# Eight-layer attention and expert kernel on one core: the last attention's batches started five steps apart, its LayerNorm and gates without exponentials, and the last experts emitted among the tails

## The chip, the cores and the metric

The kernel runs on one core of one Trainium2 chip. A core has five engines, each with its own instruction stream that it works off in order: TensorE (PE: matmuls and weight loads), VectorE (DVE), ScalarE (ACT: activation functions and copies), GpSimd (POOL), and SyncE (SP), which here only issues DMAs. They wait for each other through semaphores. The metric is the device time of one execution in microseconds (us); lower is better.

## The reference, cut to what matters

The model is four pairs of cross-attention and feed-forward over x of shape (4, 512, 128); each adds to x the result of a layer on the LayerNorm of x. The change touches the last pair (L3) only: attention over 32 context rows with 16 heads, and a top-2 mixture of 8 experts that evaluates every expert on every token.

```python
def _layernorm(x, axis=-1, eps=1e-05):
    m = jnp.mean(x, axis=axis, keepdims=True)
    v = jnp.var(x, axis=axis, keepdims=True)
    return (x - m) / jnp.sqrt(v + eps)

def _L3_xattn_ref(x, y, mask, wq, bq, wk, bk, wv, bv, wo, bo):
    ...  # q from x, k and v from y, split into 16 heads
    scores = jnp.einsum('bhqd,bhkd->bhqk', q, k) / np.sqrt(D_K)
    scores = scores + (1.0 - mask[:, None, None, :]) * -10000.0
    attn = jax.nn.softmax(scores, axis=-1)
    z = jnp.einsum('bhqk,bhkd->bhqd', attn, v)
    return z.transpose(0, 2, 1, 3).reshape(b, -1, d) @ wo.T + bo

def _L3_ffn_ref(x, router_w, w1, b1, w2, b2):
    logits = xf @ router_w.T
    probs = jax.nn.softmax(logits, axis=-1)
    top_v, top_i = jax.lax.top_k(probs, TOP_K)                      # TOP_K = 2
    gates = top_v / (jnp.sum(top_v, axis=-1, keepdims=True) + 1e-09)
    for e in range(E):                                              # E = 8
        ge = jnp.sum(jnp.where(top_i == e, gates, 0.0), axis=-1, keepdims=True)
        h = jax.nn.gelu(xf @ w1[e] + b1[e], approximate=False)
        out = out + ge * (h @ w2[e] + b2[e])

x = x + _L3_xattn_ref(_layernorm(x), ctx_1024, ...)
x = x + _L3_ffn_ref(_layernorm(x), ...)
```

## The kernel before

**Tiling.** The 2048 tokens are four batches g0 to g3 of 512 tokens; a batch is an x tile of 128 partitions by 4 token blocks (NJ) by 128 features, kept on the core throughout. Transposed activations are 128 x 512. Each of the eight PSUM tiles is 128 x 512 float32.

**Stages of the last pair.** The L2 experts end with scatters of their rows to DRAM. Then each batch goes through one chain:

- `combine2(g)`: two loads of the L2 results (tile `yg`, SP's queue), eight multiply-adds on DVE (L1152).
- `attend3(g)`, the attention: LayerNorm (statistics L194, L195 on DVE; one over the root through Ln and Exp on ACT, L199 and L200, and one Newton step on DVE, L204 to L207; the result written by ACT, L221), transposes on PE (L235) and their copy out of PSUM by ACT (L237). Then four rounds, one for each block of 128 tokens: scores (PE, L387), maximum and subtraction (DVE, L372 and L373), Exp (ACT, L374), four transposes (PE, L400), copy (ACT, L402), product with the values (PE, L406), division by the sum (DVE, L415 and L416). At the end transposes of the result (L235, L237), output projection (PE, L247) and addition to x (DVE, L459).
- `route3(g)`: LayerNorm again, this time written by DVE (L225), transposes (L235, L237), router matmul (L566), logits copied out by DVE (L572).
- `gate(g)`: top two of eight logits by comparisons on DVE, two Exps on ACT (L1196, L1197), and ten small DVE operations that make the gates.

After all four chains come the experts, batch after batch: the gates transposed (L1219, copied by ACT at L1221) and multiplied with the second biases (L247, added at L459), and then for each of eight experts two matmuls with 512 columns (L1227), two Gelus (L1228, ACT), eight matmuls of 128 columns (L1232) and four multiply-adds into x (L1242, DVE). A batch that is done is stored to `out`.

**What sets the order.** Chains are Python generators. `together` takes them in turns: in every step each running chain emits its work up to its next `yield`, and `skew` or `late` says in which step a chain starts. A scheduler then builds each engine's stream from that emission order, moving instructions where its own estimate of readiness says so. On the chip each engine works its stream off strictly in that order. In the last pair, batch g starts in step 2g (`skew` 2), and the experts are emitted by a plain loop after `together` has ended.

**ACT's function tables.** Ln and Exp are in one table set, Gelu in another. `exp_ln_tables()` loads the first at set places; the load for Gelu goes ahead of the first Gelu.

Of the kernel before, what the change touches and what calls it, by code (L numbers as in the profile page):

```python
# [8 lines left out]
F32 = mybir.dt.float32  # L9
I32 = mybir.dt.int32  # L10
# [57 lines left out]
def tile_kernel(ctx: ExitStack, tc: tile.TileContext, I, out):  # L68
# [141 lines left out]
    def normed(src, tag, plus=0.0, act=False, p=P, n=NJ, bufs=B, pool=wk):  # L210

        mv, r = yield from moments(src, p, n)
        y = pool.tile([P, n, D], F32, tag=tag, name=tag, bufs=bufs)
        if plus or act:
            c = small(n, "c")[:p]
            nc.vector.scalar_tensor_tensor(c, mv[:, :, 0], -1.0, r, ALU.mult, ALU.mult)
            if plus:
                nc.vector.tensor_scalar(c, c, plus, None, ALU.add)
        for j in range(n):
            if act:  # L220
                nc.scalar.activation(y[:p, j, :], src[:, j, :], AF.Identity, bias=c[:, j : j + 1], scale=r[:, j : j + 1])  # L221
            elif plus:
                nc.vector.tensor_scalar(y[:p, j, :], src[:, j, :], r[:, j : j + 1], c[:, j : j + 1], ALU.mult, ALU.add)
            else:
                nc.vector.tensor_scalar(  # L225
                    y[:p, j, :], src[:, j, :], mv[:, j, 0:1], r[:, j : j + 1], ALU.subtract, ALU.mult
                )
        yield
        return y
# [134 lines left out]
        nc.scalar.copy(vw[:rows], pt[:rows])  # L364
        return vw

    def softmax_terms(e, src, nh, n):

        e3 = e.rearrange("p (h n) -> p h n", n=n)
        src3 = src.rearrange("p (h n) -> p h n", n=n)  # L370
        mx = small(nh, "mx")
        nc.vector.tensor_reduce(mx, src3, AX.X, ALU.max)  # L372
        nc.vector.tensor_tensor(e3, src3, bc(mx, 2, n), ALU.subtract)  # L373
        nc.scalar.activation(e, e, AF.Exp)  # L374
        return e3

    def attend(xT, keys, values, g, H, n):
# [6 lines left out]
        for j0 in range(0, NJ, npb):  # L384
# [8 lines left out]
                )  # L393
            yield
            e = wk.tile([P, 512], F32, tag="att", name="att", bufs=B)
            softmax_terms(e, pt, npb * H, n)
            yield
            pt = psum()
            for k in range(4):
# [150 lines left out]
        return chain  # L550


    def routed(tag, w, bias=None, copies=()):


        xn, xnT = [None] * B, [None] * B
        logits = rk.tile([P, NT, NEXP], F32, tag=f"L{tag}", name="logits")

        def chain(g):
            xn[g] = yield from normed(X[g], "xn")  # L560
            for xd in copies:
                nc.sync.dma_start(xd[g * S : (g + 1) * S].rearrange("(j p) d -> p j d", p=P), xn[g])
            xnT[g] = yield from transposed(xn[g])
            pt = psum()
            for j in range(NJ):
                nc.tensor.matmul(  # L566
                    pt[:, j * P : (j + 1) * P], lhsT=xnT[g][:, j * P : (j + 1) * P], rhs=w, start=True, stop=True
                )
# [612 lines left out]
        return chain  # L1181


    def l3_ffn(xnT, logits, f3w1, f3w2, before, fetch):
        gates = [None] * B

        def gate(g):
            L = logits[:, g * NJ : (g + 1) * NJ, :]
            m1, oh1 = argmax(L, NJ)
            m2, oh2 = argmax(without(L, oh1, NJ), NJ)  # L1190

            z = rt.tile([P, NJ, NEXP], F32, tag="z", name="z", bufs=2)
            nc.vector.tensor_tensor(z, L, bc(m1, 2, NEXP), ALU.subtract)
            p2 = rt.tile([P, NJ], F32, tag="p2", name="p2", bufs=B)
            nc.vector.tensor_tensor(p2, m2, m1, ALU.subtract)
# [3 lines left out]
            p1 = rt.tile([P, NJ], F32, tag="p1", name="p1", bufs=B)  # L1199
            nc.vector.tensor_reduce(p1, z, AX.X, ALU.add)  # L1200
            nc.vector.reciprocal(p1, p1)
            nc.vector.tensor_tensor(p2, p2, p1, ALU.mult)
            den = rt.tile([P, NJ], F32, tag="den", name="den", bufs=2)
            nc.vector.scalar_tensor_tensor(den, p1, 1e-9, p2, ALU.add, ALU.add)
            nc.vector.reciprocal(den, den)
            nc.vector.tensor_tensor(p1, p1, den, ALU.mult)
            nc.vector.tensor_tensor(p2, p2, den, ALU.mult)
            gates[g] = rt.tile([P, NJ, NEXP], F32, tag="gates", name="gates", bufs=B)
            nc.vector.tensor_tensor(gates[g], oh1, bc(p1, 2, NEXP), ALU.mult)
            second = rt.tile([P, NJ, NEXP], F32, tag="second", name="second", bufs=2)  # L1210
            nc.vector.tensor_tensor(second, oh2, bc(p2, 2, NEXP), ALU.mult)
            nc.vector.tensor_tensor(gates[g], gates[g], second, ALU.add)
            yield

        together([*(queue(before(g), gate(g)) for g in range(B)), fetch], 2)
        for g in range(B):
            pt = psum()
            for j in range(NJ):
                nc.tensor.transpose(pt[:NEXP, j * P : (j + 1) * P], gates[g][:, j, :], ident)  # L1219
            gT = ex.tile([NEXP, S], F32, tag="gT", name="gT", bufs=2)  # L1220
            nc.scalar.copy(gT, pt[:NEXP])  # L1221
            add_to(X[g], proj(gT, f3b2, k=NEXP), X[g])
            for e in range(NEXP):
                hT = ex.tile([P, 2, S], F32, tag="hT", name="hT", bufs=2)
                for f in range(2):
                    pt = psum()
                    nc.tensor.matmul(pt, lhsT=f3w1[:, e, f * P : (f + 1) * P], rhs=xnT[g], start=True, stop=True)  # L1227
                    nc.scalar.activation(hT[:, f, :], pt, AF.Gelu, bias=col["f3_b1"][:, 2 * e + f : 2 * e + f + 1])  # L1228
                pt = psum().rearrange("p (j d) -> p j d", j=NJ)
                for j in range(NJ):  # L1230
                    for f in range(2):
                        nc.tensor.matmul(  # L1232
                            pt[:, j, :],
                            lhsT=hT[:, f, j * P : (j + 1) * P],
                            rhs=f3w2[:, e, f, :],
                            start=f == 0,
                            stop=f == 1,
                        )
                for j in range(NJ):
                    xj = X[g][:, j, :]  # L1240
                    ge = gates[g][:, j, e : e + 1]
                    nc.vector.scalar_tensor_tensor(xj, pt[:, j, :], ge, xj, ALU.mult, ALU.add)  # L1242
            nc.sync.dma_start(out[g].rearrange("(j p) d -> p j d", p=P), X[g])

    exp_ln_tables()
    xd0 = dram.tile([NTOK, D], F32, tag="xd0", name="xd0")
# [70 lines left out]
    with tc.tile_pool(name="lx", bufs=1) as lx:  # L1317
# [14 lines left out]

# [168 lines left out]
```

## Time and profile before

| | |
|---|---|
| median of 3 runs | 688.15 us (685.5 to 688.87) |
| the profiled execution's own time | 687.35 us |
| its span, first to last instruction | 685.5 us |
| TensorE busy / weight loads | 515.2 us (75%) / 393.8 us (57%) |
| VectorE, ScalarE, GpSimd busy | 331.9 (48%), 239.0 (35%), 164.3 us (24%) |
| mean granted TensorE clock | 0.86 |

Busy shares are means over a program of many stages, so they don't say what one stage waits for. The parts of the profile that do are: the chain that ended last, which goes back from the last instruction to what released each step; the stretches, which give each engine's busy time, and TensorE's granted clock (1.00 is full speed, 0.50 half), in any piece of the span; and the instructions in order of time, with the idle time ahead of each in brackets and what ended it. In all of them the times are us from the start of the span. Rows of PE often count twice what the source does, because a float32 matmul is recorded as two.

### The profile page before, as it was taken

How to read it: one execution, taken by the hardware profiler on the slowest of the kernel's cores; microseconds unless marked ns; L12 is line 12 of the kernel's file. 1: busy time of each engine (PE TensorE's matmuls, PEld its weight loads, DVE VectorE, ACT ScalarE, POOL GpSimd, SP SyncE). 2: the span in 40 equal slices, each digit the busy share in tenths (PEclk: the TensorE clock that was granted, in tenths of full speed). 3: DMA queues.
4: the chain of work that ended last, by engine and by line, in shares of the span. 5: the costliest groups of instructions: out<-in, count | busy, mean ns of one | idle time of the engine just before them, and what ended most of it. 6: DMA issues, size and time to landing. Idle time of an engine off the chain costs nothing.

```text
span 685.5 us, 8856 instructions
## 1 busy us (share of the span) xinstructions
PE 515.2 (75%) x3051; PEld 393.8 (57%) x3051; DVE 331.9 (48%) x1382; ACT 239.0 (35%) x540; POOL 164.3 (24%) x203
## 2 busy tenths in 40 slices
PE   3668987449389697876261997990789789999996
PEld 2557765338366436765141785880468657676765
DVE  4687654644577405666800311213867853333332
ACT  2343646203147313342110221340655334343332
POOL 4333333435012001000076766541200000000000
PEclk9999999759669889975666999996599959999999
DMA  8900101212870063002021112118000000000000
GB/s 327 313 9 17 32 27 51 77 50 73 308 277 1 0 236 134 1 1 63 0 46 43 47 47 46 38 30 257 4 1 1 1 0 1 16 0 16 1 17 15
DMA packets 42990, 44.97 MB, mean 66 GB/s; under 512 B 5161, under 2 KB 31026, under 8 KB 42818
## 3 DMA queue, kind: packets, MB, share of 16 engines
q1 hardware_dynamic: 39442, 36.20, 15.9%
q0 software_dynamic: 3072, 6.30, 3.4%
q10 hardware_dynamic: 432, 1.92, 0.8%
q8 instruction: 24, 0.39, 0.2%
q14 instruction: 20, 0.16, 0.1%
HBM read 34.97 MB, written 9.44 MB: 65 GB/s over the span
## 4 chain that ended last, share of the span: by engine, by line
PE 51%; DVE 10%; ACT 4%; issue 4%; DMA 3%; POOL 3%; another core or an unknown queue 3%; DVEq 0%; POOLq 0%; ACTq 0%
PE pt L1232 8%; PE pt L1227 8%; PE pt L1126 5%; PE pt L1118 4%; PE pt L387 3%; PE po L406 3%; PE pt L235 3%; PE pt L997 2%; PE pt L454 2%; PE pt L566 2%; POOL yd L769 2%; PE pt L400 1%; DMA yd<-ye,to 1%; PE pt L247 1%
## 5 line engine op out<-in xcount | busy, mean ns | idle before, releaser
L1232 PEld LDWEIGHTS pt<-f3w,hT 128*128 128x128 f32 x512 | 65.6, 191 | 33.4 <-ACT hT L1228 19.0
L1242 DVE SCALAR_TENSOR_TENSOR x<-pt,gates,x 128x128 f32<-128x128 f32 x128 | 36.0, 344 | 83.0 <-PE pt L1232 83.0
L1228 ACT ACTIVATE hT<-pt,cols 128x512 f32<-128x512 f32 x64 | 44.0, 688 | 73.8 <-PE pt L1227 73.4
L1232 PE MATMUL pt<-f3w,hT 128*128 128x128 f32 x512 | 68.2, 276 | 0.9 <-ACT hT L1228 0.6
L1227 PE MATMUL pt<-xnT,f3w 128*128 128x512 f32 x128 | 67.0, 611 | 0.0
L1126 PE MATMUL pt<-f2w,hT 128*128 128x128 f32 x320 | 47.2, 305 | 21.5 <-ACT hT L1121 14.6
L1121 ACT ACTIVATE hT<-pt 128x384 f32<-128x384 f32 (+1 forms) x64 | 26.9, 438 | 102.9 <-PE pt L1118 37.2
L1126 PEld LDWEIGHTS pt<-f2w,hT 128*128 128x128 f32 x320 | 44.7, 214 | 26.8 <-ACT hT L1121 15.2
L760 POOL DMA_INDIRECT xg<-xd,inv x48 | 46.5, 969 | 43.7 <-DVE to L678 14.1
L769 POOL DMA_INDIRECT yd<-ye,to x48 | 47.2, 984 | 35.6 <-DVE ye L1133 16.1
L235 PE MATMUL pt<-cst,xn 128*128 128x128 f32 x96 | 25.4, 362 | 38.7 <-ACT xn L221 20.9
L1133 DVE COPY ye<-pt 128x384 f32<-128x384 f32 (+1 forms) x16 | 7.9, 491 | 83.5 <-PE pt L1126 42.0
L235 PEld LDWEIGHTS pt<-cst,xn 128*128 128x128 f32 x96 | 15.6, 167 | 50.6 <-ACT xn L221 26.3
L194 DVE BATCH_NORM_STATS2 st<-x 128x6 f32<-128x128 f32 x128 | 32.3, 271 | 22.2 <-POOL x L547 16.1
L1118 PE MATMUL pt<-exT,f2w 128*128 128x256 f32 (+1 forms) x128 | 38.7, 445 | 0.0
L237 ACT COPY xnT<-pt 128x512 f32<-128x512 f32 x40 | 23.2, 586 | 42.5 <-PE pt L235 42.1
L400 PE MATMUL pt<-cst,att 128*128 128x128 f32 x128 | 21.0, 287 | 12.3 <-ACT att L374 12.3
L374 ACT ACTIVATE att<-att 128x512 f32<-128x512 f32 x32 | 20.0, 631 | 27.5 <-DVE att L373 27.3
L387 PE MATMUL pt<-keys,xnT 128*128 128x256 f32 (+1 forms) x64 | 28.1, 546 | 0.8 <-ACT xnT L237 0.7
L1118 PEld LDWEIGHTS pt<-exT,f2w 128*128 128x128 f32 x128 | 23.7, 196 | 7.7 <-issue 0.6
L406 PEld LDWEIGHTS po<-v,aT 128*128 128x128 f32 x192 | 25.1, 201 | 4.9 <-issue 3.5
L372 DVE TENSOR_REDUCE mx<-pt 128x16 f32<-128x512 f32 (+1 forms) x32 | 21.7, 683 | 12.8 <-PE pt L387 12.4
(323 smaller groups left out, 1024.4 us busy)
## 6 DMA issues: line engine op xcount, KB each, us to landing
e_w<-in_e_w SPq DMA_DIRECT2D x8, 512.0 KB, 7.3
e_wg<-in_e_wg SPq DMA_DIRECT2D x8, 512.0 KB, 8.0
yg<-yd SPq DMA_DIRECT2D x12, 256.0 KB, 4.2
f0w<-in_f_w SPq DMA_DIRECT2D x1, 2048.0 KB, 13.2
yd<-zero SPq DMA_DIRECT2D x8, 256.0 KB, 3.6
ew<-in_e_w SPq DMA_DIRECT2D x8, 256.0 KB, 3.2
xd<-xn SPq DMA_DIRECT2D x8, 256.0 KB, 2.2
f2w<-in_f_w SPq DMA_DIRECT2D x1, 2048.0 KB, 8.4
```

Source lines behind the costliest of these rows:

```text
L194: nc.vector.bn_stats(st[:p, j, :], src[:, j, :])
L235: nc.tensor.transpose(pt[:, j * P : (j + 1) * P], src[:, j, :], ident)
L387: nc.tensor.matmul(pt[:, j * nk : (j + 1) * nk], lhsT=xT[:, (j0 + j) * P : (j0 + j + 1) * P], rhs=keys, start=True, stop=True,)
L406: nc.tensor.matmul(po[:, k, :], lhsT=aT[:, k * P : (k + 1) * P], rhs=of(values[k % nch], cols + hpc, g), start=True, stop=True,)
L760: nc.gpsimd.indirect_dma_start(out=dst, out_offset=None, in_=table[:], in_offset=bass.IndirectOffsetOnAxis(ap=idx, axis=0))
L769: ins = nc.gpsimd.indirect_dma_start(out=table[:], out_offset=bass.IndirectOffsetOnAxis(ap=to[:, c, e : e + 1], axis=0), in_=y, in_offset=None
L1118: nc.tensor.matmul(pt[:, : m * P], lhsT=f2w1[:, e, f * P : (f + 1) * P], rhs=xT, start=True, stop=True)
L1126: nc.tensor.matmul(pt[:, c * D : (c + 1) * D], lhsT=hT[:, f, c * P : (c + 1) * P], rhs=f2w2[:, e, f, :], start=f == 0, stop=f == 3,)
L1227: nc.tensor.matmul(pt, lhsT=f3w1[:, e, f * P : (f + 1) * P], rhs=xnT[g], start=True, stop=True)
L1228: nc.scalar.activation(hT[:, f, :], pt, AF.Gelu, bias=col["f3_b1"][:, 2 * e + f : 2 * e + f + 1])
L1232: nc.tensor.matmul(pt[:, j, :], lhsT=hT[:, f, j * P : (j + 1) * P], rhs=f3w2[:, e, f, :], start=f == 0, stop=f == 1,)
L1242: nc.vector.scalar_tensor_tensor(xj, pt[:, j, :], ge, xj, ALU.mult, ALU.add)
```

## The change

Four things change, all in the last pair.

1. LayerNorm can be computed without ACT (`tables=False`): a first guess for one over the root by integer shift and subtraction of the float's bits, then three Newton steps, all on DVE. `route3` uses it; its first part has one `yield` fewer.
2. The gates use Tanh at half the argument instead of Exp, since exp(z) = (1 + tanh(z/2)) / (1 - tanh(z/2)); both Exps become one Tanh over a tile of 4 x 9. Tanh and Gelu are in the table set that is loaded here. Tanh, Gelu and the table load are all held behind the last Exp of every batch.
3. Batch g starts in step 5g instead of 2g.
4. The gates and the experts become chains of the same `together`. The experts wait until all four batches have left the attention (`attended`) and the batch's gates exist; they then emit one expert in each step. A batch's second biases follow its first expert instead of going ahead of it.

The diff, without comments and cut where it repeats:

```diff
-    def moments(src, p=P, n=NJ):
+    def moments(src, p=P, n=NJ, tables=True):
...
-        y = small(n, "y")[:p]
-        nc.scalar.activation(y, v, AF.Ln)
-        nc.scalar.activation(y, y, AF.Exp, scale=-0.5)
-        yield
-
-        t = small(n, "t")[:p]
-        nc.vector.tensor_tensor(t, y, y, ALU.mult)
-        nc.vector.scalar_tensor_tensor(t, t, -0.5, v, ALU.mult, ALU.mult)
-        r = small(n, "r")[:p]
-        nc.vector.scalar_tensor_tensor(r, t, 1.5, y, ALU.add, ALU.mult)
+        if tables:
+            y = small(n, "y")[:p]
+            nc.scalar.activation(y, v, AF.Ln)
+            nc.scalar.activation(y, y, AF.Exp, scale=-0.5)
+            yield
+        else:
+
+            i = small(n, "i", I32)[:p]
+            nc.vector.tensor_scalar(i, v.bitcast(I32), 1, None, ALU.logical_shift_right)
+            nc.vector.tensor_scalar(i, i, -1.0, float(0x5F3759DF), ALU.mult, ALU.add)
+            y = i.bitcast(F32)
+
+        for _ in range(1 if tables else 3):
+            t = small(n, "t")[:p]
+            nc.vector.tensor_tensor(t, y, y, ALU.mult)
+            nc.vector.scalar_tensor_tensor(t, t, -0.5, v, ALU.mult, ALU.mult)
+            r = small(n, "r")[:p]
+            nc.vector.scalar_tensor_tensor(r, t, 1.5, y, ALU.add, ALU.mult)
+            y = r
...
-    def softmax_terms(e, src, nh, n):
+    exps = {}
+
+    def softmax_terms(e, src, nh, n, g=None):
...
-        nc.scalar.activation(e, e, AF.Exp)
+        exps[g] = nc.scalar.activation(e, e, AF.Exp)
...
-    def l3_ffn(xnT, logits, f3w1, f3w2, before, fetch):
+    def l3_ffn(xnT, logits, f3w1, f3w2, before, route, fetch):
...
+        attended, told = [], []
+        load = []
+
+        def chain(g):
+            yield from before(g)
+            attended.append(g)
+            yield from route(g)
+            told.append(g)
+
+        def gate(g0):
+
+            while g0 not in told:
+                yield
...
-            nc.scalar.activation(z, z, AF.Exp)
-            nc.scalar.activation(p2, p2, AF.Exp)
-            yield
+            t = rt.tile([P, n, NEXP + 1], F32, tag="tanh", name="tanh", bufs=2)
+            while len(attended) < B:
+                yield
+            with after_exps():
+                nc.scalar.activation(t, z, AF.Tanh, scale=0.5)
+            yield
+            nc.vector.tensor_scalar(z, t, -1.0, 1.0, ALU.mult, ALU.add)
+            nc.vector.reciprocal(z, z)
+            nc.vector.scalar_tensor_tensor(z, t, 1.0, z, ALU.add, ALU.mult)
...
-        together([*(queue(before(g), gate(g)) for g in range(B)), fetch], 2)
-        for g in range(B):
...
+        def after_exps():
+
+            stack = ExitStack()
+            if not load:
+                with ExitStack() as behind:
+                    for g in range(B):
+                        behind.enter_context(tc.issue_after(exps[g].ins))
+                    load.append(nc.scalar.preload_act_table_set("gelu_and_others"))
+            stack.enter_context(tc.issue_after(load[0].ins))
+            return stack
...
+        def experts():
+            for g in range(B):
+                while gates[g] is None or len(attended) < B:
+                    yield
+                for e in range(NEXP):
+                    if e == 1:
+                        second_biases(g)
+                    expert(g, e)
+                    yield
+                nc.sync.dma_start(out[g].rearrange("(j p) d -> p j d", p=P), X[g])
+
+        together(
+            [*(chain(g) for g in range(B)), fetch, *(gate(g) for g in range(B)), experts()],
+            late={g: 5 * g for g in range(B)} | {B: 8} | {B + 1 + i: 0 for i in range(B + 1)},
+        )
...
-        route3, _, xnT, L = routed(3, wide["router"])
+        route3, _, xnT, L = routed(3, wide["router"], tables=False)
...
-            l3_ffn(xnT, L, f3w1, f3w2, lambda g: queue(combine2(g), attend3(g), route3(g)), fetch())
+            l3_ffn(xnT, L, f3w1, f3w2, lambda g: queue(combine2(g), attend3(g)), route3, fetch())
```

`expert(g, e)` and `second_biases(g)` hold the body of the old loop unchanged, apart from the Gelus being held behind the table load. In the built program all streams are the same as before up to the last pair, except for line numbers; within it TensorE and POOL have the same instructions as before, ACT 12 fewer and DVE 44 more. SP issues the same transfers, but of the `yg` loads the second of g2 and of g3 now go ahead of the first ones, and the last load waits for the combine of g1.

More of the change, by code (lines that the diff above doesn't have):

```diff
@@ L197, in moments, with normed @@
         nc.vector.tensor_scalar(v, mv[:p, :, 1], EPS, None, ALU.add)
-        y = small(n, "y")[:p]
-        nc.scalar.activation(y, v, AF.Ln)
-        nc.scalar.activation(y, y, AF.Exp, scale=-0.5)
-        yield
-        t = small(n, "t")[:p]
-        nc.vector.tensor_tensor(t, y, y, ALU.mult)
-        nc.vector.scalar_tensor_tensor(t, t, -0.5, v, ALU.mult, ALU.mult)
-        r = small(n, "r")[:p]
-        nc.vector.scalar_tensor_tensor(r, t, 1.5, y, ALU.add, ALU.mult)
+        if tables:
[15 more added lines that the diff above has]
+            y = r
         return mv[:p], r
-    def normed(src, tag, plus=0.0, act=False, p=P, n=NJ, bufs=B, pool=wk):
-        mv, r = yield from moments(src, p, n)
+    def normed(src, tag, plus=0.0, act=False, p=P, n=NJ, bufs=B, pool=wk, tables=True):
+        mv, r = yield from moments(src, p, n, tables)
         y = pool.tile([P, n, D], F32, tag=tag, name=tag, bufs=bufs)
@@ L395, in attend @@
             e = wk.tile([P, 512], F32, tag="att", name="att", bufs=B)
-            softmax_terms(e, pt, npb * H, n)
+            softmax_terms(e, pt, npb * H, n, g)
             yield
@@ L550, in l0_xattn, with routed @@
         return chain
-    def routed(tag, w, bias=None, copies=()):
+    def routed(tag, w, bias=None, copies=(), act=False, tables=True):
         xn, xnT = [None] * B, [None] * B
@@ L559, in chain @@
         def chain(g):
-            xn[g] = yield from normed(X[g], "xn")
+            xn[g] = yield from normed(X[g], "xn", act=act, tables=tables)
             for xd in copies:
@@ L1181, in l3_xattn @@
         return chain
-    def l3_ffn(xnT, logits, f3w1, f3w2, before, fetch):
+    def l3_ffn(xnT, logits, f3w1, f3w2, before, route, fetch):
         gates = [None] * B
[L1187 to L1195, printed above, removed]
-            nc.scalar.activation(z, z, AF.Exp)
-            nc.scalar.activation(p2, p2, AF.Exp)
-            yield
-            p1 = rt.tile([P, NJ], F32, tag="p1", name="p1", bufs=B)
-            nc.vector.tensor_reduce(p1, z, AX.X, ALU.add)
+        attended, told = [], []
[8 more added lines that the diff above has]
+                yield
+            n = NJ
+            L = logits[:, g0 * NJ : g0 * NJ + n, :]
+            m1, oh1 = argmax(L, n)
+            m2, oh2 = argmax(without(L, oh1, n), n)
+            z = rt.tile([P, n, NEXP + 1], F32, tag="z", name="z", bufs=2)
+            nc.vector.tensor_tensor(z[:, :, :NEXP], L, bc(m1, 2, NEXP), ALU.subtract)
+            nc.vector.tensor_tensor(z[:, :, NEXP], m2, m1, ALU.subtract)
+            t = rt.tile([P, n, NEXP + 1], F32, tag="tanh", name="tanh", bufs=2)
[3 more added lines that the diff above has]
+                nc.scalar.activation(t, z, AF.Tanh, scale=0.5)
+            yield
+            nc.vector.tensor_scalar(z, t, -1.0, 1.0, ALU.mult, ALU.add)
+            nc.vector.reciprocal(z, z)
+            nc.vector.scalar_tensor_tensor(z, t, 1.0, z, ALU.add, ALU.mult)
+            p1 = rt.tile([P, n], F32, tag="p1", name="p1", bufs=2)
+            nc.vector.tensor_reduce(p1, z[:, :, :NEXP], AX.X, ALU.add)
@@ L1201, in gate @@
             nc.vector.reciprocal(p1, p1)
-            nc.vector.tensor_tensor(p2, p2, p1, ALU.mult)
-            den = rt.tile([P, NJ], F32, tag="den", name="den", bufs=2)
+            p2 = rt.tile([P, n], F32, tag="p2", name="p2", bufs=2)
+            nc.vector.tensor_tensor(p2, z[:, :, NEXP], p1, ALU.mult)
+            den = rt.tile([P, n], F32, tag="den", name="den", bufs=2)
             nc.vector.scalar_tensor_tensor(den, p1, 1e-9, p2, ALU.add, ALU.add)
@@ L1207, in gate @@
             nc.vector.tensor_tensor(p2, p2, den, ALU.mult)
-            gates[g] = rt.tile([P, NJ, NEXP], F32, tag="gates", name="gates", bufs=B)
-            nc.vector.tensor_tensor(gates[g], oh1, bc(p1, 2, NEXP), ALU.mult)
-            second = rt.tile([P, NJ, NEXP], F32, tag="second", name="second", bufs=2)
+            both = rt.tile([P, n, NEXP], F32, tag="gates", name="gates", bufs=B)
+            nc.vector.tensor_tensor(both, oh1, bc(p1, 2, NEXP), ALU.mult)
+            second = rt.tile([P, n, NEXP], F32, tag="second", name="second", bufs=2)
@@ L1211, in gate @@
             nc.vector.tensor_tensor(second, oh2, bc(p2, 2, NEXP), ALU.mult)
-            nc.vector.tensor_tensor(gates[g], gates[g], second, ALU.add)
+            nc.vector.tensor_tensor(both, both, second, ALU.add)
+            gates[g0] = both
             yield
-        together([*(queue(before(g), gate(g)) for g in range(B)), fetch], 2)
-        for g in range(B):
+        def after_exps():
[7 more added lines that the diff above has]
+            return stack
@@ new lines, in expert @@
+        def expert(g, e):
+            hT = ex.tile([P, 2, S], F32, tag="hT", name="hT", bufs=2)
+            for f in range(2):
+                pt = psum()
+                nc.tensor.matmul(pt, lhsT=f3w1[:, e, f * P : (f + 1) * P], rhs=xnT[g], start=True, stop=True)
+                with after_exps():
+                    nc.scalar.activation(hT[:, f, :], pt, AF.Gelu, bias=col["f3_b1"][:, 2 * e + f : 2 * e + f + 1])
+            pt = psum().rearrange("p (j d) -> p j d", j=NJ)
+            for j in range(NJ):
+                for f in range(2):
+                    nc.tensor.matmul(
+                        pt[:, j, :],
+                        lhsT=hT[:, f, j * P : (j + 1) * P],
+                        rhs=f3w2[:, e, f, :],
+                        start=f == 0,
+                        stop=f == 1,
+                    )
+            for j in range(NJ):
+                xj = X[g][:, j, :]
+                ge = gates[g][:, j, e : e + 1]
+                nc.vector.scalar_tensor_tensor(xj, pt[:, j, :], ge, xj, ALU.mult, ALU.add)
@@ L1217, in l3_ffn, with second_biases @@
+        def second_biases(g):
             pt = psum()
@@ L1222, in l3_ffn @@
             add_to(X[g], proj(gT, f3b2, k=NEXP), X[g])
[L1223 to L1243, printed above, removed]
+        def experts():
[11 more added lines that the diff above has]
+            late={g: 5 * g for g in range(B)} | {B: 8} | {B + 1 + i: 0 for i in range(B + 1)},
+        )
     exp_ln_tables()
```

## The prediction

> **What bounds the kernel now.** I read first the chain that ended last, from the last attention on (start, length, work):
>
> ```profile
> 527.40 0.89 PE pt L247 x8
> ...
> 533.34 0.60 DVE x L459
> ...
> 551.39 1.27 PE pt L235 x4
> 552.68 0.59 ACT xnT L237
> 553.32 2.08 PE pt L566 x8
> 555.40 0.87 PE pt L1219 x4
> 556.29 0.58 ACT gT L1221
> 556.92 2.07 PE pt L247 x8
> 558.99 3.65 PE pt L1227 x4
> ```
>
> From 558.99 it is PE without a break. Ahead of that lie the tails of the batches (projection, LayerNorm, router, gates), where PE waits. Then the stretches (PE, weight loads, DVE, ACT, POOL busy, granted clock, DMA):
>
> ```profile
> 510.00:520.00 10.00, 9.90 (x64) 7.45 (x63) 7.96 (x18) 5.35 (x10) 0.00 (x0) 1.00 0.00 0
> 520.00:530.00 10.00, 10.00 (x75) 8.39 (x74) 7.14 (x21) 5.23 (x9) 0.00 (x0) 1.00 0.01 2
> 540.00:550.00 10.00, 6.05 (x33) 4.70 (x31) 8.25 (x67) 3.12 (x10) 0.00 (x0) 0.77 0.01 2
> 550.00:559.00 9.00, 6.27 (x25) 4.77 (x25) 6.54 (x51) 2.56 (x7) 0.00 (x0) 0.50 0.00 1
> 559.00:685.50 126.50, 120.97 (x676) 84.89 (x676) 39.92 (x142) 46.25 (x68) 0.00 (x0) 0.99 0.03 9
> ```
>
> With four batches interleaved PE is full from 510 to 530; from 540 to 559 it is neither full nor at full clock. The same view in finer slices shows when the clock falls and returns:
>
> ```profile
> 542.00:544.00 2.00, 1.16 (x9) 0.97 (x8) 1.28 (x12) 0.92 (x4) 0.00 (x0) 1.00 0.00 0
> 544.00:546.00 2.00, 0.26 (x2) 0.28 (x2) 2.00 (x15) 0.00 (x0) 0.00 (x0) 0.85 0.00 0
> 546.00:548.00 2.00, 1.32 (x6) 0.88 (x6) 2.00 (x17) 0.81 (x2) 0.00 (x0) 0.50 0.03 8
> ```
>
> And the instructions in order of time give the last Exp of the attention, the wait that let the clock fall, and how fast small dependent DVE operations follow each other (553.68, 553.87, 554.09: 0.2 us, where others between them cut this to about 0.085):
>
> ```profile
> 533.31 0.63 ACT L374 ACTIVATE att<-att 128x512 f32<-128x512 f32 x1 [1.33 <-DVE att L373]
> 545.74 1.15 PE L235 MATMUL pt<-cst,xn 128*128 128x128 f32 x4 [2.13 <-DVE xn L225]
> 553.68 0.15 DVE L1204 SCALAR_TENSOR_TENSOR den<-p,p 128x4 f32<-128x4 f32 x1
> 553.87 0.18 DVE L1205 RECIPROCAL den<-den 128x4 f32<-128x4 f32 x1
> 554.09 0.16 DVE L1206 TENSOR_TENSOR p<-p,den 128x4 f32<-128x4 f32 x1
> 558.32 1.28 ACT L1228 ACT_TABLE_LOAD   x1
> ```
>
> So the part that can change has three pieces: 482.90 (first scores) to 533.94 (last Exp), 51.0 us; from there to the first expert matmul, 25.05 us; and 126.5 us of experts to the end at 685.5.
>
> **Experts and their start.** The experts are held behind the last Exp, and in the built order of PE all expert matmuls stand behind the LayerNorm transposes of g3. So no expert covers a tail of g0 to g2; only the router and the gates of g3 run among experts. From the last Exp I follow the new order. The g2 transposes, held up by its Newton steps, end 3.05 us after the Exp; transposes of g3's exponentials 0.9; router of g2 at half clock (row 2.08 us for L566) to 5.95; values of g3 to 7.6 (1.91); division 0.6; transposes and copy 1.8; projection to 12; addition and statistics 2; Newton steps, 12 of them among gate operations at 0.085 and 6 alone at 0.2, 2.2; normalising 0.45 to its first quarter: 17.5 us with the hops, against 25.05: **-7.5**. Behind the first expert PE then does the router of g3 (1.3), gate transposes (0.5), the wait for their copy (1.1) and the second biases (0.9), while at the three later batch borders the first matmul of the next batch fills a Gelu wait of about 1.0, of which 0.5 stays: 3.8 - 1.5 = **+2.5** with rounding.
>
> **Smaller edits.** Per batch ACT loses Ln, Exp and two Exps (four of 0.2) and gains a Tanh (nearest row L1196, 0.23), DVE gains 11 operations: 8 for the Newton form, 3 for the gates. Of the 11, the 12-step chain counts, since in g0 to g2 PE waits for it: 7, 9 and 12 steps stand alone there, at 0.2. It is in the walk below. The shift has no row; L197 (0.16) is nearest. DVE's gates of g0 and g1 wait for their Tanhs, and behind them on DVE stand the logits of g2 and the division of g3, which TensorE needs; the Tanhs are done 1.8 us after the last Exp, DVE is busy with g2's LayerNorm until 2.7, so this costs nothing. The table load was on ACT at 558.32 for 1.28 us, in the open only beside PE's matmuls; now it follows the last Exp, and the next copy is wanted 3.1 us later. The Trainium skill (ScalarE: Activation LUTs, What ACT_TABLE_LOAD costs) puts a switch at 2.66 us with a drain; with two Tanhs that too just fits in 3.1. Without that cover it would cost 1.3 by the row, 2.7 by the page. The loads of yg: SP's order puts second halves of g2 and g3 first, and the last load waits for g1's combine at 480; a load lands in 4.2 us (row of yg), DVE wants it after 500. Hidden. POOL's order is unchanged.
>
> **The stagger is the main term.** One round of a lone batch at full clock: scores 1.02, maximum 0.69, subtraction 0.69, Exp 0.63, transposes 0.60, copy 0.59, values 0.89, seven hops of 0.05: 5.45 us; at half clock scores are 2.08, transposes 1.1, values 1.7: 7.9. Two-step stagger kept four batches in rounds together; five steps (a round has four) leave g0 alone for a round, g0 and g1 for a round, and g2, g3 at the end. That alone would be bearable. But streams are strict, and in the new PE order the LayerNorm transposes of one batch stand ahead of another batch's ready work: those of g2 ahead of g0's third round, of g0 ahead of g1's last transposes and g3's second scores, of g1 ahead of g2's last, of g2 ahead of g3's last. Each waits for addition, statistics, Newton steps and normalising on DVE, with other batches' maxima and subtractions between them.
>
> I walked the new order by hand with these rows. g0's scores start at 482.9, 490.6, about 500 and 513.5 (half clock at first, alone; then 3 us of PE idle because g2's normalising on ACT stands behind an Exp of g1). g3's start at 521, 533, 543.5 and 558.4; last Exp at 562.3. One period as an example, g1's addition to g2's, 16.6 us: addition and statistics 1.6, maxima and subtractions for g2 and g3 3.15, Newton steps 1.8, first normalised quarter 0.4; on PE transposes 1.0, transposes of g2's exponentials 0.6, router 1.7, values 1.7, transposes 0.85 and 0.95, values 1.7, projection 1.05. PE's idle gaps before the three LayerNorm transposes come out at 3.5, 4.5 and 5.0 us.
>
> Last Exp 562.3 instead of 533.9: **+28.4**. Sum: 28.4 - 7.5 + 2.5 = +23.4. In the walk I let the clock come back late; half of that returned is -3. Span 685.5 + 20.4 = 706; the profiled execution took 1.85 more than its span, and the median shown is 0.8 above that execution: **708 us**.
>
> **Clock rule against row.** The skill (TensorE: Matmul & The Clock Gate, Part 1) says the clock is set by activity in free-running windows of about 3.4 us, and falls after an idle window. By it the three gaps cool PE, but the earlier one of 3.0 (with g2's first transposes) would not. The row has a gap of 2.13 between sparse work that did it (545.74, clock 0.50 after), and the clock came back only in 562 to 564. I take the row; the rule alone would give 3 us less, 705. A PE that stays at full clock in all four gaps saves 14 of the walk: about 3 behind 508, 3.5 behind 532, 4 behind 549, 3.5 behind 564.
>
> **Rivals.** (a) The same entanglement, warm clock: 709 - 14 = 695 span, 697.5 us. For it: a stage around 264 to 284 has PE busy 2.7 of 4 us at clock 1.00; against it: gaps here are longer. (b) Faster: the tails don't hold the rounds up, because DVE gets through them between the rounds. Then the last Exp comes after 30 steps of 5.45/4, some 42 us after 482.9: 525, 9 earlier; with -7.5 and +2.5 the span is 671.5, 674 us. It decides at a last Exp below 539: earlier means faster. For it: DVE is only 71 to 80% busy between 510 and 530. Against: PE's order. (c) A wash: half of the stagger's loss is taken up, last Exp near 539, 685 to 691. (d) Worse than the walk: gaps add up and nothing warms before the experts, 717 and up, as more hops slip.
>
> **How the numbers follow.** Main case 0.62 (own range 700 to 717), (a) 0.17 (690 to 702), (b) 0.09, (c) 0.06, (d) 0.06. 0.5% of 688 is 3.4 us, about what a measurement tells from no change. Faster 0.09, same 0.06, slower 0.85. The range reaches from (a)'s lower end to the main case's upper: 690 to 717; (b), most of (c) and (d) are left out.
>
> **What would show it.** Last Exp (attention, ACT) near 560, and 17 us from there to the first matmul of the experts; PE rows of the LayerNorm transposes with 3 to 5 us idle ahead, released by DVE's xn; clock at 0.5 in slices between 530 and 575; four rounds of g3 11 to 15 us apart; experts about 129 us. Wrong if the last Exp is below 540, if the PE idle ahead of these transposes is under 1 us, or if the clock stays at 1.00 through them.

## The result, and the profile after

The changed kernel takes 706.05 us (median; 704.93 to 710.74) where the kernel before takes 688.15: the ratio is 1.027, with an interval of 1.023 to 1.0311. It is slower. The profiled execution took 704.93 us with a span of 703.1, so 17.6 more than the 687.35 and 685.5 of before.

Nothing happened ahead of the change: the first transposes of the last attention start at 481.39 (480.60 before). From there on, in three pieces:

| us | first transposes to end of last Exp | to first expert matmul | to the end | sum |
|---|---|---|---|---|
| before | 53.3 | 25.05 | 126.5 | 204.9 |
| after | 75.8 | 15.8 | 130.2 | 221.7 |
| difference | +22.5 | -9.3 | +3.7 | +16.8 |

The instructions of the kernel after in order of time (start, length, engine, line; in brackets the idle time ahead and what ended it):

```profile
504.87 0.86 PE L244 MATMUL pt<-cst,xn 128*128 128x128 f32 x2 [2.98 <-ACT xn L230]
528.45 0.30 PE L244 MATMUL pt<-cst,xn 128*128 128x128 f32 x1 [3.19 <-DVE xn L234]
544.83 1.15 PE L244 MATMUL pt<-cst,xn 128*128 128x128 f32 x4 [4.72 <-DVE xn L234]
...
556.52 0.63 ACT L385 ACTIVATE att<-att 128x512 f32<-128x512 f32 x1 [4.91 <-DVE att L384]
557.16 1.28 ACT L1254 ACT_TABLE_LOAD   x1
...
559.26 1.15 PE L244 MATMUL pt<-cst,xn 128*128 128x128 f32 x4 [5.21 <-DVE xn L234]
571.98 1.15 PE L244 MATMUL pt<-cst,xn 128*128 128x128 f32 x4 [5.02 <-DVE xn L234]
```

These five are the only waits of TensorE of 1 us or more between 490 and 574. The last four are the transposes of the last LayerNorm, for g0, g1, g2 and g3. TensorE reaches them 3 to 5 us before DVE has written the rows that they transpose, and as its stream is strict, everything behind them waits too, the scores of g3's last round (553.03) among it, and with them the last Exp. The waits between 525 and 580 add up to this (us in all, times, longest):

```profile
PE pt L244 <- DVE xn L234: 18.1, 4, 5.2
```

18.1 us, of which the 5.0 ahead of g3's lie behind the last Exp and the other 13.1 ahead of or beside it. The stretches (PE, weight loads, DVE, ACT, POOL busy, granted clock, DMA) show the same from the side of the engines:

```profile
520.00:530.00 10.00, 6.81 (x44) 5.47 (x43) 7.97 (x36) 3.09 (x6) 0.00 (x0) 0.94 0.00 0
530.00:540.00 10.00, 9.84 (x59) 7.22 (x57) 6.85 (x30) 3.25 (x6) 0.00 (x0) 0.89 0.01 2
540.00:550.00 10.00, 5.28 (x27) 4.82 (x27) 6.04 (x28) 2.43 (x4) 0.00 (x0) 0.66 0.00 1
550.00:560.00 10.00, 4.63 (x30) 3.33 (x28) 8.43 (x41) 3.37 (x6) 0.00 (x0) 0.81 0.00 0
560.00:573.00 13.00, 6.88 (x39) 5.91 (x39) 11.61 (x79) 1.89 (x4) 0.00 (x0) 0.76 0.00 1
573.00:703.10 130.10, 123.89 (x697) 87.14 (x696) 43.08 (x159) 46.91 (x70) 0.00 (x0) 0.99 0.03 9
```

From 540 to 573 TensorE is about half busy, with the attention still running until 557. Neither TensorE nor DVE is full there: they wait for each other in turns. The chain that ended last shows one such turn (start, length, work):

```profile
544.83 1.15 PE pt L244 x4
...
552.30 0.91 PE pt L256 x8
...
553.30 0.70 DVE x L470
...
555.79 0.69 DVE att L384
...
556.59 0.18 DVE i L206
...
558.57 0.17 DVE r L215
...
558.77 0.36 DVE xn L234
559.13 0.14 issue
559.26 1.15 PE pt L244 x4
```

Behind g1's transposes stands work of TensorE and ACT, ending with the projection of g2; then the chain runs for 5.5 us on DVE alone, from g2's addition at 553.30 over its statistics, a maximum and subtraction for g3 (555.79) and eleven dependent operations of the Newton form (556.59 to 558.74) to the normalising; and only then TensorE again, with g2's transposes.

### The profile page after: what moved, and what is told of

It is laid out like the page before. It is cut to its first block, busy times and chain, and to the rows that moved or that the text cites. A ratio compares the mean times of both kernels' runs of the same rounds, so it can differ in the third digit from the quotient of the medians.

```text
span 703.1 us, 8871 instructions
## 1 busy us (share of the span) xinstructions
PE 516.8 (74%) x3051; PEld 393.8 (56%) x3051; DVE 342.3 (49%) x1426; ACT 235.9 (34%) x528; POOL 164.0 (23%) x203
## 4 chain that ended last, share of the span: by engine, by line
PE 43%; DVE 13%; POOL 7%; issue 6%; ACT 4%; DMA 3%; another core or an unknown queue 3%; DVEq 0%; POOLq 0%; ACTq 0%
PE pt L1268 8%; PE pt L1262 8%; POOL yd L780 4%; PE pt L244 3%; PE pt L398 3%; PE po L417 3%; PE pt L1129 2%; PE pt L1137 2%; PE pt L1008 2%; POOL xg L771 2%; PE pt L465 2%; DVE st L194 2%; PE pt L411 2%; PE pt L577 1%
## 5 line engine op out<-in xcount | busy, mean ns | idle before, releaser
L244 PE MATMUL pt<-cst,xn 128*128 128x128 f32 x96 | 25.4, 370 | 52.9 <-DVE xn L234 31.0
L1137 PE MATMUL pt<-f2w,hT 128*128 128x128 f32 x320 | 45.5, 298 | 22.5 <-ACT hT L1132 15.7
L1137 PEld LDWEIGHTS pt<-f2w,hT 128*128 128x128 f32 x320 | 42.9, 205 | 28.0 <-ACT hT L1132 16.7
L246 ACT COPY xnT<-pt 128x512 f32<-128x512 f32 x40 | 23.2, 586 | 54.7 <-PE pt L244 54.6
L411 PE MATMUL pt<-cst,att 128*128 128x128 f32 x128 | 22.9, 303 | 12.4 <-ACT att L385 12.3
L417 PE MATMUL po<-v,aT 128*128 128x128 f32 x192 | 28.4, 294 | 1.7 <-ACT aT L413 1.7
```

Of the source, the lines that this page charges most:

```text
L244: nc.tensor.transpose(pt[:, j * P : (j + 1) * P], src[:, j, :], ident)
L411: nc.tensor.transpose(pt[:, k * P : (k + 1) * P], e[:, k * P : (k + 1) * P], ident)
L417: nc.tensor.matmul(po[:, k, :], lhsT=aT[:, k * P : (k + 1) * P], rhs=of(values[k % nch], cols + hpc, g), start=True, stop=True,)
L1137: nc.tensor.matmul(pt[:, c * D : (c + 1) * D], lhsT=hT[:, f, c * P : (c + 1) * P], rhs=f2w2[:, e, f, :], start=f == 0, stop=f == 3,)
```

## The experiments

The runs were made in four groups, of four, four, three and one. In the last two, the stages ahead of the last pair took some 20 us less in all kernels than in the first two (first transposes of the last attention at 455.7 to 464.2 instead of 479.3 to 485.1), and the kernel before took 664.5 to 664.8 us instead of 689 to 690; no run says why. So I compare ratios to the kernel before within a group, and lengths counted from those first transposes. Each length is of one profiled execution; two executions in which the clock came back at different times differed by some 2 us (see the run with added matmuls below), so smaller differences mean little.

### The stagger and the rest, each alone

The kernel after with the old stagger:

```diff
-            late={g: 5 * g for g in range(B)} | {B: 8} | ...
+            late={g: 2 * g for g in range(B)} | {B: 8} | ...
```

> The changed kernel with the batches two steps apart again; all else of the change stays. Theory (the stagger is the main term, the rest of the change gains): last Exp of the attention near 534 as before, 16 to 20 us from there to the first expert matmul, experts 130 us: about 685 us, 3 below before. Rival (the LayerNorm and gates on DVE, or the experts' place, cost the time): it stays at 700 or above.

698.62 us, ratio 1.0114 (1.0058 to 1.017). A miss: without the stagger the other edits don't gain, they cost. The attention is back at its old length (53.6 us to the last Exp), but from there to the first expert it is 29.5 us instead of 25.05, and the experts take 130.1. The tails come one after the other, and TensorE waits in each:

```profile
539.09 0.32 PE L244 MATMUL pt<-cst,xn 128*128 128x128 f32 x1 [3.37 <-DVE xn L234]
...
548.26 0.30 PE L244 MATMUL pt<-cst,xn 128*128 128x128 f32 x1 [3.36 <-DVE xn L234]
...
557.55 1.16 PE L244 MATMUL pt<-cst,xn 128*128 128x128 f32 x4 [3.92 <-DVE xn L234]
...
566.62 1.15 PE L244 MATMUL pt<-cst,xn 128*128 128x128 f32 x4 [4.50 <-DVE xn L234]
```

The reverse, the kernel before with the new stagger alone:

```diff
-        together([*(queue(before(g), gate(g)) for g in range(B)), fetch], 2)
+        together([*(queue(before(g), gate(g)) for g in range(B)), fetch], late={g: 5 * g for g in range(B)} | {B: 8})
```

> The kernel before with the batches five steps apart and nothing else changed. Theory: the last Exp comes near 555 to 560 and the tail to the first expert matmul stays at 20 to 25 us, so 705 to 712 us, as slow as the whole change or slower. Rival (the stagger is harmless and the loss comes from the longer chain on DVE): within 1% of before, 682 to 695 us.

704.94 us, ratio 1.0221 (1.0172 to 1.027), at the lower end of the expected. From the first transposes: 70.3, 20.1 and 127.9 us, 13.4 more than before. In this run, with the old LayerNorm, the long waits ahead of the router's LayerNorm transposes are two, 1.86 and 4.47 us; between them TensorE waits for Exps, ahead of the attention's own transposes:

```profile
539.57 0.66 PE L400 MATMUL pt<-cst,att 128*128 128x128 f32 x4 [3.00 <-ACT att L374]
551.83 1.11 PE L400 MATMUL pt<-cst,att 128*128 128x128 f32 x4 [3.80 <-ACT att L374]
```

So the stagger alone costs 13.4, the rest alone 8.3 (213.2 against 204.9), and both together 16.8, less than the sum of 21.7: they lose in part the same time.

### Is it the order, or the clock?

The same instructions as in the kernel after, but the transposes are asked for four turns later, so that other batches' work comes ahead of them in TensorE's stream. What follows them in their chain (copy, router, gates) moves with them:

```diff
             xn[g] = yield from normed(X[g], "xn", act=act, tables=tables)
             ...
+            for _ in range(0 if tables else 4):
+                yield
             xnT[g] = yield from transposed(xn[g])
```

> The changed kernel, stagger five, with four more yields ahead of the last LayerNorm's transposes, so that in TensorE's order other batches' ready work, and for the last batch two or three experts, stand ahead of them; the work is the same. Theory (TensorE's strict order makes DVE's LayerNorm chain hold up ready work): the idle time of 18 us ahead of these transposes falls below 5, last Exp near 543, first expert some 9 us later, about 686 us. Rival (lone batches in their rounds are the loss, whatever the order): last Exp stays above 553, and the time at 697 or above.

688.91 us, ratio 0.9977 (0.9953 to 1.0001): the whole loss is gone, with not one instruction fewer. The transposes stand where their rows are ready, and no wait is left ahead of those of any batch. These are g0's, g1's and g2's, and g3's, which now stand among the experts:

```profile
540.11 0.60 PE L244 MATMUL pt<-cst,xn 128*128 128x128 f32 x4
...
548.99 0.60 PE L244 MATMUL pt<-cst,xn 128*128 128x128 f32 x4
...
559.15 0.60 PE L244 MATMUL pt<-cst,xn 128*128 128x128 f32 x4
...
576.16 0.60 PE L244 MATMUL pt<-cst,xn 128*128 128x128 f32 x4
```

```profile
540.00:550.00 10.00, 8.70 (x59) 6.54 (x57) 9.14 (x52) 3.80 (x7) 0.00 (x0) 1.00 0.00 1
550.00:561.30 11.30, 7.47 (x43) 6.12 (x44) 10.08 (x71) 4.13 (x8) 0.00 (x0) 0.85 0.00 0
```

The last Exp ends at 552.25, much later than the 543 I had expected and just below the 553 of the rival ("lone batches in their rounds are the loss"). The first expert follows 9.1 us behind it, as expected (15.8 in the kernel after), since it no longer stands behind g3's transposes. From the first transposes it is 67.1, 9.1 and 128.9: 205.1 us, as before the change. So the new order takes 8.7 us off the attention and 6.7 off what follows, but the attention is still 13.8 us longer than in the kernel before (53.3): the total is made up behind the last Exp, not in the rounds.

That run also has a warmer clock. So the other half of the question: keep TensorE warm and leave the order. Four matmuls of 512 columns (eight in the records) on old data, whose result nobody reads, stand ahead of each batch's transposes:

```diff
+            if not tables:
+                pt = psum()
+                for _ in range(4):
+                    nc.tensor.matmul(pt, lhsT=ident, rhs=..., start=True, stop=True)
             xnT[g] = yield from transposed(xn[g])
```

> The changed kernel with four more matmuls of 512 columns ahead of each of the last LayerNorm's transposes, into a PSUM tile that nobody reads; they fill idle TensorE time. Theory (the idle gaps also cost clock): granted clock stays at 1.00 through the gaps of the tails, which saves 6 to 9 us of matmuls at half clock: about 699 us. Rival (clock plays no part, DVE's chain sets the pace): 704 to 708 us, or later by the matmuls' own time.

705.07 us, ratio 1.0216 (1.0154 to 1.0278); 221.3 us from the first transposes against 221.7. The clock is back from 530 to 560, and the total is the same:

```profile
540.00:550.00 10.00, 7.67 (x36) 4.58 (x35) 6.98 (x31) 2.33 (x4) 0.00 (x0) 1.00 0.00 1
550.00:560.00 10.00, 8.39 (x43) 5.22 (x41) 8.32 (x42) 3.44 (x6) 0.00 (x0) 1.00 0.00 0
560.00:575.00 15.00, 12.37 (x44) 8.65 (x44) 11.57 (x82) 1.79 (x4) 0.00 (x0) 0.66 0.01 2
```

But the same total does not mean that the clock costs nothing, for this execution lost time at both ends. Ahead of the first added matmul TensorE's rows stand in the same order in both runs; yet here the clock came back later (0.50 at 498 to 500 and at 511 to 513, where the kernel after has 1.00 at the same distance from the first transposes), and g3's first transposes come 36.5 us after g0's (519.31 against 482.81), not 34.3: 2.2 us later, and I see no other difference. And ahead of g3's transposes in the last LayerNorm the clock fell all the same (14.9 us from g2's to g3's, 12.7 in the kernel after). In between, g1's and g2's transposes still wait for DVE, behind the added work:

```profile
546.77 0.30 PE L244 MATMUL pt<-cst,xn 128*128 128x128 f32 x1 [1.27 <-DVE xn L234]
560.25 0.30 PE L244 MATMUL pt<-cst,xn 128*128 128x128 f32 x1 [1.78 <-DVE xn L234]
```

From g0's to g1's it is 14.7 us (16.4 in the kernel after), from g1's to g2's 13.5 (14.4). So at full clock a period is 0.9 to 1.7 us shorter, with the rows of two batches interleaved a little differently; the 5.5 us of DVE in it (553.30 to 558.77 above, 554.28 to 559.76 here) stay. Two warm periods give 2.6 us, far from the 16.6 that the order gave. What warmth through all four gaps would give isn't shown.

### What in the rest costs

The kernel before with the Newton form of the kernel after in the router's LayerNorm, and nothing else of the change (gates, experts and stagger as before):

```diff
-        route3, _, xnT, L = routed(3, wide["router"])
+        route3, _, xnT, L = routed(3, wide["router"], tables=False)
```

> The kernel before with one edit: the last LayerNorm (the one ahead of the router) without Ln and Exp, three Newton steps on DVE in their place; stagger of two, gates and expert loop as before. Theory (dependent small DVE operations, 0.2 us apart, lie on the path of every tail): 8 more such operations, 1.6 us, less Ln, Exp and their hops, about 0.6, so 1.0 a tail, and four tails follow each other: +4, about 694 us beside 690 for the kernel before. Rival (what the edits cost without the stagger comes from the gates and the new place of the experts, not from the Newton form): 690, within 1.

700.32 us, ratio 1.0197 (1.0141 to 1.0254). More than either theory: it adds 10.7 us (215.6 from the first transposes), all of it between last Exp and first expert (35.5 us instead of 25.05). In TensorE's rows in order of time something is seen that eleven small operations can't explain:

```profile
546.53 0.30 PE L244 MATMUL pt<-cst,xn 128*128 128x128 f32 x1 [3.20 <-DVE xn L234]
546.67 0.39 PE L256 MATMUL pt<-w,oT 128*128 128x128 f32 x2
...
551.29 0.62 PE L244 MATMUL pt<-cst,o 128*128 128x128 f32 x4
555.47 0.45 PE L244 MATMUL pt<-cst,xn 128*128 128x128 f32 x1 [3.56 <-DVE xn L234]
555.71 0.64 PE L256 MATMUL pt<-w,oT 128*128 128x128 f32 x2
```

The projection of the next batch (L256) is interleaved with the transposes of the one before, and so waits with them. Its addition, statistics and Newton steps can start only when it is done. The transposes of the four tails follow each other one by one, 9.0 us apart (537.52, 546.53, 555.47, 564.52). In the kernel before the projections stood ahead (537.28, 542.46), between other batches' transposes. The form without Ln and Exp has one `yield` fewer, and that turn was what had put the transposes behind the projection. So, the same with the turn kept:

```diff
             y = i.bitcast(F32)
+            yield
```

> The kernel before with the Newton form alone, as before, but with the turn kept at which the old form handed on to the other batches (the Ln and the Exp ended in one). The arithmetic is that of the run without it. Theory (the 10 us that the Newton form cost alone come from the lost turn: the transposes of one batch's LayerNorm move ahead of the next batch's projection in TensorE's order, so the tails follow each other one by one, 9.0 us apart): most of it comes back, 690 to 694. Rival (eleven dependent DVE operations in a row are what costs): 698 to 701, as without the turn.

Ratio 1.0022 (1.0006 to 1.0039; 665.57 us where before takes 664.47), and 206.9 us from the first transposes, 2.0 more than before. Arithmetic and instructions are those of the run above; the turn alone is worth 8.7 us between the two profiled executions (12 by the two ratios, which come from different groups). The rows now have the projection of one batch ahead of the transposes of the other:

```profile
523.14 1.91 PE L257 MATMUL pt<-w,oT 128*128 128x128 f32 x8
524.85 1.92 PE L416 MATMUL po<-v,aT 128*128 128x128 f32 x8
526.55 0.94 PE L245 MATMUL pt<-cst,xn 128*128 128x128 f32 x4
...
529.17 1.06 PE L257 MATMUL pt<-w,oT 128*128 128x128 f32 x8
534.10 1.15 PE L245 MATMUL pt<-cst,xn 128*128 128x128 f32 x4 [3.87 <-DVE xn L235]
```

How much the dependent operations themselves cost in the kernel after, where they do stand on the path:

```diff
-        for _ in range(1 if tables else 3):
+        for _ in range(1):
```

> The kernel after with one Newton step in place of three; two steps are left out, so the inverse root is only a rough one and the output is off by that. 6 DVE operations fewer in each tail, all of them dependent on each other. If the waits of TensorE for the normalised rows (18.1 us in four, from the end of the third round on) are made of this chain, each falls by 1.2 and the time by 5 to 6: 699 to 700. If they are made of where the transposes stand in TensorE's order, with other batches' maxima and subtractions between on DVE, at most 2 us go: 703 to 705.

699.98 us, ratio 1.0206 (1.014 to 1.0272). TensorE's four waits fall from 18.1 to 13.4 us, by 1.2 each as the first theory had it: six operations at 0.2.

```profile
PE pt L244 <- DVE xn L234: 13.4, 4, 4.0
```

The rest of each wait stays. The time is less clear: 699.98 is what the first theory expected, but the ratio makes 702.3 on a kernel before of 688.15, between the two, and its interval overlaps with that of the kernel after. From the first transposes it is 217.9 us, 3.8 less than in the kernel after.

The turn, kept in the kernel after (same edit as in the run with the turn above, stagger five):

> The kernel after with that one turn kept, stagger of five. If one turn is enough to let the next batch's ready work past the transposes, most of the 17 us comes back as with four turns: 689 to 694. If with this stagger the work that should stand ahead comes two or more turns later, the waits of TensorE ahead of the transposes shrink only by part: 697 to 703. If the turn plays no part at this stagger: 705 to 707.

Ratio 1.0196 (1.0155 to 1.0238), which makes 701.6 on a kernel before of 688.15: by part, as the second case has it. The four waits are 3.30, 2.66, 0.95 and 1.95 us, and two waits for an Exp have come in (1.52 and 3.25 us). From the first transposes it is 217.0 us, 4.7 less than in the kernel after. One turn lets only some of the ready work past.

### A version that beats both

If the order is what costs, the idea of the change (experts among the tails) may still be good. Stagger two and four turns:

> The kernel after with a stagger of two and the transposes of the last LayerNorm asked for four turns later. Theory (TensorE's order: a transpose that isn't ready stops ready work behind it): the four waits of 3.4 to 4.5 us that remained at a stagger of two are filled, 698.6 less 8 to 12: 687 to 691. Rival (in the tails DVE, 75 to 86% busy, sets the pace, and no order of TensorE changes that): 696 to 699.

684.55 us, ratio 0.9943 (0.992 to 0.9967): 0.6% faster than before, and more than expected. With a stagger of three:

> The same with a stagger of three. If tails and rounds can cover each other once TensorE's order lets them, this is the best of the four (two, three, five steps): 683 to 688. If the rounds need four batches side by side to keep TensorE full, it lies between two and five: 688 to 691.

680.79 us, ratio 0.9901 (0.9866 to 0.9936), the lowest ratio of all, as the first case had it. From the first transposes 57.8, 7.5 and 131.5: 196.8 us. The experts start at 546.98, while g2's transposes (549.12) and g3's (564.42) are still to come, and TensorE is 86 to 100% busy and warm through it:

```profile
540.00:550.00 10.00, 8.64 (x59) 6.68 (x59) 9.65 (x68) 4.44 (x8) 0.00 (x0) 1.00 0.01 2
550.00:560.00 10.00, 9.11 (x57) 6.54 (x56) 8.61 (x59) 2.60 (x6) 0.00 (x0) 1.00 0.00 1
560.00:570.00 10.00, 10.00 (x62) 7.42 (x61) 6.44 (x34) 4.65 (x8) 0.00 (x0) 1.00 0.00 0
```

Stagger four, four turns:

> The kernel after with a stagger of four and the transposes four turns later; two gave 684.6 and three 680.8, five 688.9. If the stagger has its best at three because four batches side by side keep TensorE full and tails still get covered: 682 to 686. If the number of steps is not what matters and each order is a matter of luck: outside of that.

Ratio 1.0069 (1.0047 to 1.0092), a miss: worse than two, three and five. It is the attention that is long (74.0 us to the last Exp, 57.8 with three). TensorE's rows show the transposes of the exponentials of two batches back to back, and waiting for an Exp, and the products with the values of four batches in one block (32 records; a batch has 8):

```profile
491.50 1.25 PE L411 MATMUL pt<-cst,att 128*128 128x128 f32 x8 [3.08 <-ACT att L385]
...
501.32 1.17 PE L411 MATMUL pt<-cst,att 128*128 128x128 f32 x8 [1.21 <-ACT att L385]
...
504.54 5.02 PE L417 MATMUL po<-v,aT 128*128 128x128 f32 x32
...
515.58 1.25 PE L411 MATMUL pt<-cst,att 128*128 128x128 f32 x8 [1.68 <-ACT att L385]
```

A round has four turns, so batches four steps apart do the same thing in the same turn. The rows fit that; no run tests it by itself. Last, stagger three with the one turn in place of four:

> The kernel after with a stagger of three and only the one lost turn kept in the last LayerNorm (with four turns and a stagger of three the ratio was 0.990). One turn brought back nearly all at a stagger of two with the old tails, and a quarter at five. If with three steps the next batch's ready work stands within one turn, the ratio is 0.988 to 0.998; if more turns are needed because the gates' operations and other batches' rounds lie between, TensorE waits 2 to 4 us ahead of the transposes and the ratio is 1.005 to 1.015.

Ratio 1.0008 (0.9992 to 1.0023), between the two cases expected. TensorE still waits 2.26, 2.96 and 2.51 us ahead of the transposes of g0 to g2.

All of it in one table, us from the first transposes to the end, each from one execution. Rows: turns at which the transposes let others past, counted from the kernel after:

| | stagger 2 | 3 | 4 | 5 |
|---|---|---|---|---|
| no turn | 213.2 (215.6 with old gates and experts) | | | 221.7 |
| one turn | 206.9 (old gates and experts) | 205.4 | | 217.0 |
| four turns | 201.2 | 196.8 | 212.4 | 205.1 |

The kernel before is at 204.9 in it, with two steps, one turn and the old form.

## Why the prediction was right, and where its reasons were not

**The sum.** Predicted span 706, measured 703.1. Last Exp: predicted at 562.3, with 3 back for the clock, so +25.4; measured 557.15 against 533.94, +23.2. Last Exp to first expert: -7.5 predicted, -9.3 measured. Experts: +2.5 predicted, +3.7 measured. The three errors are -2.2, -1.8 and +1.2. The walk's g3 scores (521, 533, 543.5, 558.4) were at 521.0, 529.8, 539.1 and 553.0: right at the start, and then the three rounds, walked at 12.0, 10.5 and 14.9 us, took 8.8, 9.3 and 13.9. Inside the sum, 3.8 - 1.5 is 2.3 and not 2.5, and g3's values at 5.95 plus the row's 1.91 end at 7.9 and not at 7.6; in rival (b), 30 steps of 1.36 are 41 us and not 42. None of these moves the result by more than 1.1 us. That the total came within 3 us is partly luck: the half of the clock's return that was taken off was a guess, and errors of both signs cancel.

**The mechanism.** The step that held is "streams are strict, and in the new PE order the LayerNorm transposes of one batch stand ahead of another batch's ready work". The gaps of 3.5, 4.5 and 5.0 us were 3.19, 4.72 and 5.21, released by DVE's `xn`, and moving those transposes, with what follows them in their chain, gave the time back.

**"The stagger is the main term"** holds, but not as the whole. Alone it costs 13.4 us; on top of the rest 8.5 (221.7 against 213.2). The rest costs 8.3 alone and 3.4 on top of the stagger (221.7 against 218.3), where I had priced it as 11 operations on DVE and had expected a small gain once the stagger was gone. And with the stagger alone, about half of TensorE's long waits stand ahead of other transposes than the ones that I named, those of the exponentials (3.00 and 3.80 us, beside 1.86 and 4.47). The step that failed is "Smaller edits": it priced the Newton form by its operations and left out the turn that went with the Ln and the Exp. By the two runs with the Newton form alone, at a stagger of two, the turn is worth 8.7 us and the operations 2.0 (1.5 by the ratio, 0.4 to 2.7). In the kernel after, the turn is worth 4.7 and six of the operations 3.8. The order that I walked held the lost turn, so the total came out right; the account of which edit pays for it did not.

**The clock.** The rows have it at 0.50 behind all these gaps, as predicted, and the earlier one of 2.98 us cooled it too:

```profile
504.00:506.00 2.00, 1.13 (x5) 0.75 (x5) 1.97 (x10) 1.97 (x5) 0.00 (x0) 0.74 0.00 0
506.00:508.00 2.00, 1.75 (x6) 1.09 (x5) 1.64 (x11) 1.34 (x4) 1.41 (x1) 0.50 0.00 0
```

There the row was the better guide than the reading of the Trainium skill (TensorE: Matmul & The Clock Gate, Part 1) by which a gap of 3.0 would not. But the price was too high where the runs can test it: 3 to 4 us for each gap, 14 in all, as rival (a) has it. In the two periods in which the run with added matmuls kept TensorE warm, it gained 1.7 and 0.9. DVE's 5.5 us in each period stay what they are.

**The table load** took 1.28 us behind the last Exp (557.16), and the Tanhs followed at 558.46. It hid, as the row had said; a price of 2.66 for the switch (ScalarE: Activation LUTs, What ACT_TABLE_LOAD costs) is not seen in this place.

**Rival (b)'s border**, a last Exp below 539, was set too low. With four turns the last Exp came at 552.25 and the kernel was as fast as before, because the first expert then follows in 9.1 us and not in 17.5, g3's transposes having moved among the experts. "No expert covers a tail of g0 to g2" is true of this kernel's order, and not of the change as such: with a stagger of three, experts do.

**Experts.** 130.2 us for the 129 implied. With the new loop they took 128.8 us or more in every run, with the old one 125.5 to 127.9. How much of that is the new place of the biases, and how much the router of g3 among the experts, wasn't separated.

## What to carry to other kernels

When a generator or planner sets the order of strict streams, a turn that is dropped with an instruction is an edit of its own: compare the built order of the bounding engine, and ask for each operation that waits what ready work stands behind it. Here moving each batch's LayerNorm transposes by four turns was worth 17 us, with the same instructions, and the same idea with that order and a stagger of three was 1% faster than the kernel before. The number of turns has to fit the stagger: with a stagger of four the same move left the kernel 0.7% slower than before. Before a low clock is blamed, look at how much of the period is the clocked engine's own work; and before two runs of equal time are taken to show that the clock costs nothing, compare them piece by piece.

## What the runs showed of the hardware

Small operations on DVE that depend on each other follow at 0.2 us though each takes 0.16 (in the kernel after, 558.18, 558.37, 558.57). With independent ones between them all instructions start about 0.1 us apart, and the dependent ones stay at about 0.2 (569.05, 569.25 and 569.46 in g3's Newton steps, with gate operations at 569.15 and 569.37 between). So a second chain fits into the gaps of the first at little cost. Six of the dependent ones taken out of each of TensorE's four waits shortened these by 4.7 us in all.

In the kernel after, the granted clock was 0.50 behind each gap of 2.98 to 5.21 us. With the clock kept at 1.00, periods of 16.4 and 14.4 us, of which DVE alone holds 5.5, were 1.7 and 0.9 us shorter. And of two executions with the same order of TensorE's rows, the one in which the clock came back later was 2.2 us behind after some 35 us.
